# A four-layer metaformer on one core: the expert biases of layer 1 as bfloat16 parts, and one product for the ranks below the diagonal

## The chip, the cores and the metric

The kernel runs on one core of a Trainium2 chip. The metric is the device time of one execution in microseconds; lower is better. A core has five engines with queues of their own: TensorE (PE; its weight loads are listed as PEld), VectorE (DVE), ScalarE (ACT), GpSimd (POOL), and SyncE (SP), which issues most of the transfers. They run side by side and wait for each other by semaphores. Data are worked on in SBUF, 128 partitions wide; TensorE writes its products to PSUM.

## The reference

The program sends 4 x 64 images of 128 x 128 values (256 images) through four layers, each a mixer and a feed-forward part. The change is in layer 1 (the code counts from 0), the second of the four. Its mixer gives every pair (n, m) of rows in an image a weight by the rank of its score among all 128 x 128 scores of the image, and its feed-forward part sends each row to 2 of 8 experts:

```python
ranks = (jnp.argsort(tau, axis=-1) + 1).astype(score.dtype) / n
weights = -jnp.log(ranks).reshape(shp)
...
router_probs = jax.nn.softmax(x @ router_w + router_b, axis=-1)
top_p, top_i = jax.lax.top_k(router_probs, K)
top_p = top_p / jnp.sum(top_p, axis=-1, keepdims=True)
expert_out = jnp.einsum('bnd,edc->bnec', x, expert_w) + expert_b
gathered = jnp.take_along_axis(expert_out, top_i[..., None], axis=2)
return jnp.einsum('bnk,bnkc->bnc', top_p, gathered)
```

So a row's result is the sum over its two experts of gate x (row x expert matrix + expert bias). Everything is float32.

## The kernel before

The layers follow one another through arrays in DRAM. Layer 1 first finds the ranks (distances, then a long sort, lines L1453 to L1833) and leaves them in DRAM as integers, one half of each rank matrix above and one below the diagonal, with a list of tied ranks. Then `l1_blocks` (L1838) does everything else of the layer. It works on 32 blocks of 8 images; most steps are done once for each half block of 4 images, so 64 times.

What a block does, in order of its data:
- `load` and `load_ranks` (L2183, L2187) fetch 8 images and their ranks through SP's queue; `cast` (L2193, GpSimd) turns the ranks into the f32 tiles `above` and `below`.
- `normed` (L1915 to L1981) normalises the images and turns them over by products with the identity.
- `attention`: `tied` (L1991, L1992, VectorE) makes two bfloat16 tiles `ta` and `tb` that place the tied ranks; `ranks` (L1994) adds up the rank matrix of each image in the PSUM tile `pt`: `below` times the identity (L1997), `above` turned over (L1998), and `ta` times `tb` (L1999). All the products of one image follow one another before the next image's. `log` takes the logarithm to `wT`, `values` (L2009) and `product` (L2021) apply the weights, `add` (L2029, L2032) adds to the image.
- `gates`: `route` (L2049) gives the logits; VectorE computes softmax and the choice of two (L2068 to L2091), and `split` (L2094) writes the gates of 8 experts as three bfloat16 parts that add up to the float32 value, `g3` of 3 x 8 values per row.
- `experts`: `turn` (L2114, products L2118) brings the 24 values of each row to 24 partitions, PSUM tile `pl`; ScalarE copies them twice: `keep` to the bfloat16 tile `gb`, `keep_too` (L2126) to the f32 tile `gf`. `spread` (L2137), once for each of the 8 experts, copies an expert's gate to all partitions, as a product of `gb` with the 0/1 matrix `pick`. `times` (L2147) multiplies the images by it: five experts on VectorE, straight from PSUM, three on GpSimd after a copy by ScalarE (L2143). `mixed` (L2159), once per image, adds up in the PSUM tile `pe` the bias, `gf` times `eb3` (L2163: the biases three times over, one for each part of the gate), and the eight products with the expert matrices (L2165). `add` (L2170) adds it to the image, and the block is stored (L2207).

A product of f32 operands stands in the trace as two MATMUL instructions, two passes, each with a weight load; one of bfloat16 operands as one.

The order on TensorE, ScalarE, VectorE and GpSimd isn't that of the code. Each step is given to a planner (`Plan`, L49) with its engine, a cost in microseconds written by hand, the tiles it reads and writes, and those it takes anew. `emit` (L94) goes through them as a list scheduler: always the step that can start first by these costs, given the number of buffers of every tile. The order that results is fixed in the program. By the written costs a block takes 37.6 us of TensorE and 35.0 us of VectorE. Buffers that matter here: `pt` and `pr` two, `pl`, `pv`, `po` and `pe` one each (all PSUM), `xg`, `gb` and `gf` two, and three of most tiles of a block.

Ahead of the blocks lies a setup (L1846 to L1896) that loads the weights through SP's queue, in this order with the blocks' first loads, and makes constants: among them `eb3` (L1875 to L1877), `ones3` and `pick` (L1887 to L1891).

Of the kernel before, what the change touches and what calls it, by code (L numbers as in the profile page):

```python
# [10 lines left out]
F32 = mybir.dt.float32  # L11
I32 = mybir.dt.int32
# [3 lines left out]
BF16 = mybir.dt.bfloat16  # L16
AF = mybir.ActivationFunctionType
ALU = mybir.AluOpType
# [4 lines left out]
P = 128  # L23
B, H, W, C = 4, 64, 128, 128
# [24 lines left out]
class Plan:  # L49
# [16 lines left out]
    def step(self, engine, us, reads, writes, fn, new="", late=0.0):  # L66

        i, deps, holds = len(self.steps), set(), []
        for n in new.split():

            self.last[n] = [set(), None, set()]
            self.users.append((n, self.last[n][0]))
            holds.append(len(self.users) - 1)
            if n in self.turns:
                self.turns[n].append(holds[-1])
        for n in reads.split():
            t = self.last[n]
            t[0].add(i)
            if t[1] is not None:
                deps.add(t[1])  # L80
            t[2].add(i)
        for n in writes.split():
            t = self.last.setdefault(n, [set(), None, set()])
            t[0].add(i)
            deps |= t[2]
            if t[1] is not None:
                deps.add(t[1])
            t[1], t[2] = i, set()
        for n in new.split():
            self.last[n][0].add(i)  # L90
        deps.discard(i)
        self.steps.append((engine, us, deps, holds, fn, late))
# [1745 lines left out]
def l1_blocks(env, x, out, pk, ties, cv, ff):  # L1838

    nc, tc = env.nc, env.tc  # L1840
    NB, E = 8, 8
    with tc.tile_pool(name="ec", bufs=1) as cp, tc.tile_pool(name="es", bufs=3) as sb, tc.tile_pool(
        name="ep", bufs=1, space=PSUM
# [6 lines left out]
        eb = cp.tile([P, 2], F32, name="eb")  # L1850
# [21 lines left out]
        ew = cp.tile([P, E, C], F32, name="ew")  # L1872
        nc.sync.dma_start(ew, ff["expert_w"].rearrange("e d c -> d e c"))

        eb3 = cp.tile([3 * E, C], F32, name="eb3")  # L1875
        for k in range(3):
            nc.sync.dma_start(eb3[E * k : E * k + E, :], ff["expert_b"])  # L1877

        below = cp.tile([P, E, E], F32, name="below")
        nc.vector.memset(below, 0.0)  # L1880
        for i in range(1, E):
# [1 line left out]

        identb = cp.tile([P, P], BF16, name="identb")
        nc.vector.tensor_copy(identb, env.ident)
        ones3 = cp.tile([P, 3, E], F32, name="ones3")
        nc.vector.tensor_copy(ones3, env.ident[:, 0:E].unsqueeze(1).to_broadcast([P, 3, E]))  # L1887
        pp = ps1.tile([3 * E, P], F32, name="pl")
        nc.tensor.matmul(pp, ones3.rearrange("p k e -> p (k e)"), env.ident, start=True, stop=True)
        pick = cp.tile([3 * E, E, P], BF16, name="pick")  # L1890
        nc.vector.tensor_copy(pick, pp[:, 0:E].unsqueeze(2).to_broadcast([3 * E, E, P]))  # L1891
        places = cp.tile([P, P], I32, name="places")
        nc.gpsimd.iota(places, [[1, P]], base=0, channel_multiplier=0)  # L1893
        placeb = cp.tile([P, P], BF16, name="placeb")
# [5 lines left out]
        deep = ["xt", "xT", "xT2", "e", "g", "g3", "mx", "sm", "sn"]  # L1900
        deep += [n + k for n in ("st", "mv", "rs", "nb", "d", "t") for k in "12"]
        plan = Plan(dict(
            gate=DEEP, rt=2, above=2, below=2, xl=2, wT=2, v=2, gt=1, xg=2, gb=2, gf=2, gr=2, ws=2, ta=2, tb=2,
            pt=2, pv=1, po=1, pl=1, pr=2, pe=1, **{n: DEEP for n in deep},
        ), "ta tb wT v gate rt above below xg gb gf gt " + " ".join(deep))
        step = plan.step

        def normed(v, k, tags, eps, name):
# [74 lines left out]
        def attention(v, j0):  # L1983
            w = {}

            def tied():
                w["ta"] = sb.tile([P, 4, P], BF16, name="ta", bufs=2)
                w["tb"] = sb.tile([P, 4, P], BF16, name="tb", bufs=2)
                for j in range(4):
                    col, row, lack = (ties[:, k, v["i"] + j0 + j : v["i"] + j0 + j + 1] for k in range(3))  # L1990
                    V.tensor_scalar(w["ta"][:, j, :], placeb, col, None, ALU.is_equal)  # L1991
                    V.tensor_scalar(w["tb"][:, j, :], placeb, row, lack, ALU.is_equal, ALU.mult)  # L1992

            def ranks():  # L1994
                w["pt"] = ps2.tile([P, 4, P], F32, name="pt")
                for j in range(4):
                    T.matmul(w["pt"][:, j, :], env.ident, v["below"][:, j0 + j, :], start=True, stop=False)  # L1997
                    T.matmul(w["pt"][:, j, :], v["above"][:, j0 + j, :], env.ident, start=False, stop=False)  # L1998
                    T.matmul(w["pt"][:, j, :], w["ta"][:, j, :], w["tb"][:, j, :], start=False, stop=True)  # L1999

            def log():

                w["wT"] = sb.tile([P, 4, P], F32, name="wT", bufs=2)
                S.activation(w["wT"], w["pt"], AF.Ln, scale=1.0 / (W * W))

            def values():
                w["pv"] = ps1.tile([P, 4, C], F32, name="pv")
                for j in range(4):
                    T.matmul(w["pv"][:, j, :], v["xT"][:, j0 + j, :], m, start=True, stop=True)  # L2009

            def keep():

                w["v"] = sb.tile([P, 4, C + 1], F32, name="v", bufs=2)
                G.memset(w["v"][:, :, C : C + 1], 1.0)
                V.tensor_add(w["v"][:, :, 0:C], w["pv"], cst.unsqueeze(1).to_broadcast([P, 4, C]))

            def product(j):
                def f():
                    w["po", j] = ps1.tile([P, 2, 2 * P], F32, name="po")
                    for q in range(2):  # L2020
                        T.matmul(  # L2021
                            w["po", j][:, q, 0 : C + 1], w["wT"][:, j + q, :], w["v"][:, j + q, :], start=True, stop=True
                        )
                return f

            def add(j):
                def f():
                    po, ws = w["po", j], sb.tile([P, 2], F32, name="ws", bufs=2)
                    V.reciprocal(ws, po[:, :, C])  # L2029
                    for q in range(2):  # L2030
                        xj = v["xt"][:, j0 + j + q, :]
                        V.scalar_tensor_tensor(xj, po[:, q, 0:C], ws[:, q : q + 1], xj, ALU.mult, ALU.add)  # L2032
                return f

            step("dve", 1.4, "above", "ta tb", tied, new="ta tb")
            step("pe", 2.4, "above below ta tb", "pt wT", ranks, new="pt wT")
            step("act", 0.6, "pt", "wT", log)
            step("pe", 1.0, "xT_%d" % j0, "pv v", values, new="pv v")
            step("dve", 0.75, "pv", "v", keep)
            for j in range(0, 4, 2):  # L2040
                step("pe", 0.5, "wT v", "po", product(j), new="po")
                step("dve", 0.95, "po xl0 xl4 xm0 xm4", "x1_%d ws" % (j0 + j), add(j), new="ws")

        def gates(v):
# [49 lines left out]
            def split():  # L2094

                g = v["g"]
                v["g3"] = g3 = sb.tile([P, NB, 3, E], BF16, name="g3")
                V.tensor_copy(g3[:, :, 0, :], g)
                V.tensor_sub(g, g, g3[:, :, 0, :])
                V.tensor_copy(g3[:, :, 1, :], g)  # L2100
                V.tensor_sub(g3[:, :, 2, :], g, g3[:, :, 1, :])

            step("dve", 0.5, "", "e mx", shift, new="mx")
            step("act", 0.35, "", "e", lambda: S.activation(v["e"], v["e"], AF.Exp))
# [5 lines left out]
        def experts(v, j0):  # L2110
# [2 lines left out]

            def turn():  # L2114
                w["xg"] = sb.tile([P, E, 4, P], F32, name="xg", bufs=2)
                w["pg"] = ps1.tile([3 * E, 4, P], F32, name="pl")
                for j in range(4):
                    T.matmul(  # L2118
                        w["pg"][:, j, :], v["g3"][:, j0 + j].rearrange("p k e -> p (k e)"), identb, start=True, stop=True
                    )  # L2120

            def keep():
                w["gb"] = sb.tile([3 * E, 4, P], BF16, name="gb", bufs=2)
                S.copy(w["gb"], w["pg"])

            def keep_too():  # L2126
                w["gf"] = sb.tile([3 * E, 4, P], F32, name="gf", bufs=2)
                S.copy(w["gf"], w["pg"])

            step("pe", 0.6, "g3", "pl xg", turn, new="pl xg")  # L2130
            step("act", 0.55, "pl", "gb", keep, new="gb")
            step("act", 0.55, "pl", "gf", keep_too, new="gf")

            def spread(q):
                def f():
# [23 lines left out]
            def mixed(j):  # L2159
                def f():  # L2160
                    if j == 0:
                        w["pe"] = ps1.tile([P, 4, C], F32, name="pe")
                    T.matmul(w["pe"][:, j, :], w["gf"][:, j, :], eb3, start=True, stop=False)  # L2163
                    for q in range(E):
                        T.matmul(w["pe"][:, j, :], w["xg"][:, q, j, :], ew[:, q, :], start=False, stop=(q == E - 1))  # L2165
                return f

            def add():
# [2 lines left out]

            parts = " ".join("xg%d_%d" % (j0, q) for q in range(E))
            for j in range(4):
                step("pe", 2.1, "xg gf " + parts, "pe", mixed(j), new="pe" if j == 0 else "")
            step("dve", 0.7, "pe x1_%d x1_%d xl0 xl4 xm0 xm4" % (j0, j0 + 2), "x2_%d" % j0, add)

        def block(i):
# [1259 lines left out]
```

## Time and profile before

| | |
|---|---|
| median of 3 runs | 12128.36 us (12107.32 to 12131.01) |
| the profiled execution, its own time | 12125.25 us |
| its span, first to last instruction | 12123.1 us |
| mean granted TensorE clock | 0.789 of full |
| busy, whole span | PE 62%, DVE 83%, ACT 62%, POOL 51% |
| stage of the blocks | 5331 to 6715 us |
| largest groups on PE there | L2165 536.0 us busy (x4096), L2137 177.6 (x512), L1997 114.7 (x512), L2163 113.6 (x512) |

The profile is of one execution. Busy time counts an instruction from start to end; the ends of matmuls are modelled and overlap their followers, so where TensorE is tight the distances between starts are the better measure. "out<-in" names the tiles that a group writes and reads; 24*128 after the tiles of a matmul are the rows and columns of the array that it uses. The clock column is the share of full TensorE clock that was granted.

### The profile page before, as it was taken

To read this page: it belongs to the slowest core of one execution; us is meant where nothing else is said; L and a number is where in the kernel's file an instruction comes from. 1 tells how busy PE (TensorE), PEld (TensorE's weight loads), DVE (VectorE), ACT (ScalarE), POOL (GpSimd) and SP (SyncE) were. 2 spreads that over 40 slices of the span, in tenths; PEclk is the share of its full clock that TensorE was granted. 3 is DMA by queue.
4 is the path that set the end of the run, shared out by engine and by line. 5 is a ranking of instruction groups with operands and counts; after the bars stand their busy time and mean duration, and the time that the engine had idled before them with its cause. 6 is when DMAs were issued, how large, how long until landed. Compare 5 with 4: busy or idle time off the path is not lost. (4 is left out here: it accounts for less than half of the span.)

```text
span 12123.1 us, 115274 instructions
## 1 busy us (share of the span) xinstructions
PE 7529.4 (62%) x34606; PEld 4567.5 (38%) x34606; DVE 10007.7 (83%) x16341; ACT 7550.9 (62%) x10927; POOL 6180.6 (51%) x5275
## 2 busy tenths in 40 slices
PE   7887785000000000038999699999899999998765
PEld 5655554000000000027788344444444444446443
DVE  7566638999999999987787699999999999997354
ACT  4355534888867777622333577787777777786332
POOL 1000016999950000002222699999989999995222
PEclk8876798555555555569999899999999999999877
DMA  4223245111111111121111233434333433433434
GB/s 142 83 46 94 72 143 136 56 58 57 58 55 56 56 56 53 40 54 37 38 40 30 103 138 137 142 137 149 133 138 137 141 135 140 144 134 116 177 124 155
DMA packets 632306, 1193.55 MB, mean 98 GB/s; under 512 B 216508, under 2 KB 433902, under 8 KB 552302
## 3 DMA queue, kind: packets, MB, share of 16 engines
q1 hardware_dynamic: 587454, 1042.99, 25.7%
q0 software_dynamic: 34656, 140.92, 3.5%
q8 instruction: 279, 4.57, 0.2%
q10 hardware_dynamic: 9552, 2.08, 0.1%
q14 instruction: 365, 2.99, 0.1%
HBM read 950.86 MB, written 251.71 MB: 99 GB/s over the span
## 5 line engine op out<-in xcount | busy, mean ns | idle before, releaser
L2699 POOL TENSOR_TENSOR gs<-hist,cc 128x512 f32<-128x512 f32 x2048 | 2573.5, 1265 | 382.4 <-DVE hist L2694 237.8
L2694 DVE TENSOR_TENSOR_SCAN hist<-da,state,bs 128x512 f32<-128x512 f32 x1984 | 2524.0, 1272 | 0.0
L2708 PE MATMUL py<-gs,ident 128*128 128x512 f32 x4096 | 2248.1, 631 | 5.8 <-DVE y L2584 5.8
L1633 PE MATMUL pt<-ident,both 128*128 128x128 f32 x6 | 2.7, 445 | 3258.3 <-DVE both L1631 3258.3
L2665 ACT ACTIVATE da<-dt,am 128x512 f32<-128x512 f32 x2048 | 1415.0, 715 | 332.6 <-DVE hist L2694 330.0
L2686 DVE TENSOR_TENSOR bs<-dx,bs 128x512 f32<-128x512 f32 x2048 | 1393.7, 681 | 182.6 <-PE bs L2672 136.1
L1509 POOL TENSOR_TENSOR diff<-key 128x2048 f32<-128x2048 f32 (+11 forms) x364 | 1384.1, 3861 | 87.1 <-DVE key L1514 75.1
L1633 PEld LDWEIGHTS pt<-ident,both 128*128 128x128 f32 x6 | 1.1, 182 | 3259.8 <-issue 3259.8
L2708 PEld LDWEIGHTS py<-gs,ident 128*128 128x128 f32 x4096 | 739.1, 197 | 905.4 <-issue 427.3
L1893 POOL IOTA places<- 128x128 int32 x1 | 0.2, 239 | 1811.4 <-SPq L1833 1811.4
L2672 PE MATMUL bs<-bt,pick 96*128 96x512 bf16 x2048 | 807.2, 394 | 145.1 <-DVE hist L2694 142.1
L1531 ACT COPY keep<-rank 128x1536 int16<-128x1536 int16 (+11 forms) x364 | 612.8, 1686 | 437.5 <-DVE rank L1533 388.8
L1507 ACT COPY low<-key 128x2048 f32<-128x2048 f32 (+11 forms) x364 | 627.7, 1725 | 285.1 <-DVE key L1514 276.0
L1532 DVE COPY_PREDICATED rank<-back,rank 128x1536 int16<-128x1536 uint8 (+11 forms) x364 | 781.6, 2147 | 16.7 <-ACT keep L1531 16.7
L1533 DVE COPY_PREDICATED rank<-back,keep 128x1536 int16<-128x1536 uint8 (+11 forms) x364 | 777.9, 2137 | 12.5
L1513 DVE TENSOR_TENSOR key<-low,key 128x2048 f32<-128x2048 f32 (+11 forms) x364 | 749.3, 2059 | 6.9 <-DMA key<-dist 4.4
L1514 DVE TENSOR_TENSOR key<-low,key 128x2048 f32<-128x2048 f32 (+11 forms) x364 | 744.5, 2045 | 12.4
L1510 ACT ACTIVATE turned<-diff 128x2048 int8<-128x2048 f32 (+11 forms) x364 | 600.5, 1699 | 36.5 <-DMA key<-dist 27.4
L1522 ACT ACTIVATE back<-turned 128x3072 uint8<-128x3072 int8 (+12 forms) x182 | 582.5, 3200 | 0.0
L2165 PE MATMUL pe<-ew,xg 128*128 128x128 f32 x4096 | 536.0, 285 | 1.7 <-DVE xg L2147 1.7
L2165 PEld LDWEIGHTS pe<-ew,xg 128*128 128x128 f32 x4096 | 486.0, 195 | 34.0 <-DVE xg L2147 2.5
L2147 POOL TENSOR_TENSOR xg<-xT,gr 128x512 f32<-128x512 f32 x192 | 245.3, 1278 | 473.1 <-ACT gr L2143 472.9
(815 smaller groups left out, 18624.6 us busy)
## 6 DMA issues: line engine op xcount, KB each, us to landing
cc<-cd SPq DMA_DIRECT2D x512, 1024.0 KB
xt<-state SPq DMA_DIRECT2D x64, 1024.0 KB
xo<-state SPq DMA_DIRECT2D x128, 256.0 KB
state<-xo POOLq DMA_DIRECT2D x128, 256.0 KB, 2.8
xl<-in_L_ffn_weight SPq DMA_DIRECT2D x32, 1024.0 KB
tk<-in_x SPq DMA_DIRECT2D x32, 512.0 KB
tokens<-tt POOLq DMA_DIRECT2D x32, 512.0 KB, 4.8
tk<-tokens SPq DMA_DIRECT2D x8, 2048.0 KB
```

The source lines that it names most:

```text
L1509: nc.gpsimd.tensor_sub(d, lo[part], hi[part])
L1513: nc.vector.tensor_tensor(lo[part], c, hi[part], ALU.min)
L1514: nc.vector.tensor_tensor(hi[part], c, hi[part], ALU.max)
L1532: nc.vector.copy_predicated(l, t, h)
L1533: nc.vector.copy_predicated(h, t, kv)
L2165: T.matmul(w["pe"][:, j, :], w["xg"][:, q, j, :], ew[:, q, :], start=False, stop=(q == E - 1))
L2665: nc.scalar.activation(da, x_["dt%d" % b], AF.Exp, scale=am[:, s : s + 1])
L2672: nc.tensor.matmul(bs, pick[:, s, :], x_["bt%d" % b], start=True, stop=True)
L2686: nc.vector.tensor_mul(db, x_["dx%d" % b], db)
L2694: nc.vector.tensor_tensor_scan(h, live.pop(("da", t)), live.pop(("db", t)), 0.0 if first else state[b][:, s : s + 1], ALU.mult, ALU.add,)
L2699: nc.gpsimd.tensor_tensor(gs, h, live.pop(("cc", t)), ALU.mult)
L2708: nc.tensor.matmul(x_["py%d" % b], env.ident, live.pop(("gs", t)), start=(s == 0), stop=(s == S - 1))
```

## The change

Three things are edited, all in `l1_blocks`.

Biases. `eb3` (f32, 24 rows) becomes `eb9` (bfloat16, 72 rows): each bias is split into three bfloat16 parts that add up to it, and part l stands in rows 24 l to 24 l + 23, three times over. It is made in the setup, from nine loads of `expert_b` in place of three and some 15 small instructions. `split` writes the three parts of the gates three times, so that every part of a gate meets every part of a bias; `turn`, `gb` and `pick` get 72 rows in place of 24 (the rows of `pick` from 24 on are zero, so `spread` computes what it did). The f32 copy `gf` and its step are gone. `mixed` adds the bias of all four images as four bfloat16 products ahead of the first image's expert products, and the accumulation in `pe` is begun once and ended once for the four.

Ranks. `below` times the identity is one product of 512 columns for the four images in place of four of 128; then come the four of `above`, then the four of `ta` and `tb`.

Planner. The cost of `ranks` is 2.2 in place of 2.4, `keep_too` is gone, and `mixed` waits for `gb` in place of `gf`.

```diff
-        eb3 = cp.tile([3 * E, C], F32, name="eb3")
-        for k in range(3):
-            nc.sync.dma_start(eb3[E * k : E * k + E, :], ff["expert_b"])
+        R = 9 * E
+        eb9 = cp.tile([R, C], BF16, name="eb9")
+        with tc.tile_pool(name="eb", bufs=1) as bp:
...
+            for k in range(9):
+                nc.sync.dma_start(left[E * k : E * k + E, :], ff["expert_b"])
+            row = bp.tile([R, 1], I32, name="row")
+            nc.gpsimd.iota(row, [[1, 1]], base=0, channel_multiplier=1)
...
+            for l in range(3):
+                nc.vector.tensor_copy(part, left)
+                nc.vector.tensor_sub(left, left, part)
+                nc.vector.scalar_tensor_tensor(ebs, part, sel[:, l : l + 1], ebs, ALU.mult, ALU.add)
+            nc.vector.tensor_copy(eb9, ebs)
...
-        pick = cp.tile([3 * E, E, P], BF16, name="pick")
-        nc.vector.tensor_copy(pick, pp[:, 0:E].unsqueeze(2).to_broadcast([3 * E, E, P]))
+        pick = cp.tile([R, E, P], BF16, name="pick")
+        nc.vector.tensor_copy(pick, pp[:, 0:E].unsqueeze(2).to_broadcast([R, E, P]))
...
             def ranks():
                 w["pt"] = ps2.tile([P, 4, P], F32, name="pt")
+                T.matmul(w["pt"], env.ident, v["below"][:, j0 : j0 + 4, :], start=True, stop=False)
                 for j in range(4):
-                    T.matmul(w["pt"][:, j, :], env.ident, v["below"][:, j0 + j, :], start=True, stop=False)
                     T.matmul(w["pt"][:, j, :], v["above"][:, j0 + j, :], env.ident, start=False, stop=False)
-                    T.matmul(w["pt"][:, j, :], w["ta"][:, j, :], w["tb"][:, j, :], start=False, stop=True)
+                for j in range(4):
+                    T.matmul(w["pt"][:, j, :], w["ta"][:, j, :], w["tb"][:, j, :], start=False, stop=(j == 3))
...
-            step("pe", 2.4, "above below ta tb", "pt wT", ranks, new="pt wT")
+            step("pe", 2.2, "above below ta tb", "pt wT", ranks, new="pt wT")
...
-                v["g3"] = g3 = sb.tile([P, NB, 3, E], BF16, name="g3")
-                V.tensor_copy(g3[:, :, 0, :], g)
-                V.tensor_sub(g, g, g3[:, :, 0, :])
-                V.tensor_copy(g3[:, :, 1, :], g)
-                V.tensor_sub(g3[:, :, 2, :], g, g3[:, :, 1, :])
+                gs = g.unsqueeze(2).to_broadcast([P, NB, 3, E])
+                v["g3"] = g3 = sb.tile([P, NB, 3, 3, E], BF16, name="g3")
+                V.tensor_copy(g3[:, :, :, 0, :], gs)
+                V.tensor_sub(g, g, g3[:, :, 0, 0, :])
+                V.tensor_copy(g3[:, :, :, 1, :], gs)
+                V.tensor_sub(g3[:, :, :, 2, :], gs, g3[:, :, :, 1, :])
...
-                w["gb"] = sb.tile([3 * E, 4, P], BF16, name="gb", bufs=2)
+                w["gb"] = sb.tile([R, 4, P], BF16, name="gb", bufs=2)
                 S.copy(w["gb"], w["pg"])
...
-            step("act", 0.55, "pl", "gf", keep_too, new="gf")
...
                     if j == 0:
                         w["pe"] = ps1.tile([P, 4, C], F32, name="pe")
-                    T.matmul(w["pe"][:, j, :], w["gf"][:, j, :], eb3, start=True, stop=False)
+                        for q in range(4):
+                            T.matmul(w["pe"][:, q, :], w["gb"][:, q, :], eb9, start=(q == 0), stop=False)
                     for q in range(E):
-                        T.matmul(w["pe"][:, j, :], w["xg"][:, q, j, :], ew[:, q, :], start=False, stop=(q == E - 1))
+                        T.matmul(w["pe"][:, j, :], w["xg"][:, q, j, :], ew[:, q, :], start=False, stop=(j == 3 and q == E - 1))
...
-                step("pe", 2.1, "xg gf " + parts, "pe", mixed(j), new="pe" if j == 0 else "")
+                step("pe", 2.1, "xg gb " + parts, "pe", mixed(j), new="pe" if j == 0 else "")
```

More of the change, by code (lines that the diff above doesn't have):

```diff
@@ L1873, in l1_blocks @@
         nc.sync.dma_start(ew, ff["expert_w"].rearrange("e d c -> d e c"))
-        eb3 = cp.tile([3 * E, C], F32, name="eb3")
-        for k in range(3):
-            nc.sync.dma_start(eb3[E * k : E * k + E, :], ff["expert_b"])
+        R = 9 * E
+        eb9 = cp.tile([R, C], BF16, name="eb9")
+        with tc.tile_pool(name="eb", bufs=1) as bp:
+            left, part, sel = bp.tile([R, C], F32, name="left"), bp.tile([R, C], BF16, name="part"), bp.tile([R, 3], F32, name="sel")
+            ebs = bp.tile([R, C], F32, name="ebs")
+            for k in range(9):
+                nc.sync.dma_start(left[E * k : E * k + E, :], ff["expert_b"])
+            row = bp.tile([R, 1], I32, name="row")
+            nc.gpsimd.iota(row, [[1, 1]], base=0, channel_multiplier=1)
+            rowf = bp.tile([R, 1], F32, name="rowf")
+            nc.vector.tensor_copy(rowf, row)
+            nc.vector.tensor_scalar(sel[:, 0:1], rowf, float(3 * E), None, ALU.is_lt)
+            nc.vector.tensor_scalar(sel[:, 2:3], rowf, float(6 * E), None, ALU.is_ge)
+            nc.vector.tensor_tensor(sel[:, 1:2], sel[:, 0:1], sel[:, 2:3], ALU.add)
+            nc.vector.tensor_scalar(sel[:, 1:2], sel[:, 1:2], -1.0, 1.0, ALU.mult, ALU.add)
+            nc.vector.memset(ebs, 0.0)
+            for l in range(3):
[3 more added lines that the diff above has]
+            nc.vector.tensor_copy(eb9, ebs)
         below = cp.tile([P, E, E], F32, name="below")
@@ L1885, in l1_blocks @@
         nc.vector.tensor_copy(identb, env.ident)
[L1886 to L1889, printed above, removed]
-        pick = cp.tile([3 * E, E, P], BF16, name="pick")
-        nc.vector.tensor_copy(pick, pp[:, 0:E].unsqueeze(2).to_broadcast([3 * E, E, P]))
+        ones9 = cp.tile([P, 9, E], F32, name="ones9")
+        nc.vector.memset(ones9, 0.0)
+        nc.vector.tensor_copy(ones9[:, 0:3, :], env.ident[:, 0:E].unsqueeze(1).to_broadcast([P, 3, E]))
+        pp = ps1.tile([R, P], F32, name="pl")
+        nc.tensor.matmul(pp, ones9.rearrange("p k e -> p (k e)"), env.ident, start=True, stop=True)
+        pick = cp.tile([R, E, P], BF16, name="pick")
+        nc.vector.tensor_copy(pick, pp[:, 0:E].unsqueeze(2).to_broadcast([R, E, P]))
         places = cp.tile([P, P], I32, name="places")
@@ L1902, in l1_blocks @@
         plan = Plan(dict(
-            gate=DEEP, rt=2, above=2, below=2, xl=2, wT=2, v=2, gt=1, xg=2, gb=2, gf=2, gr=2, ws=2, ta=2, tb=2,
+            gate=DEEP, rt=2, above=2, below=2, xl=2, wT=2, v=2, gt=1, xg=2, gb=2, gr=2, ws=2, ta=2, tb=2,
             pt=2, pv=1, po=1, pl=1, pr=2, pe=1, **{n: DEEP for n in deep},
-        ), "ta tb wT v gate rt above below xg gb gf gt " + " ".join(deep))
+        ), "ta tb wT v gate rt above below xg gb gt " + " ".join(deep))
         step = plan.step
@@ L2115, in turn @@
                 w["xg"] = sb.tile([P, E, 4, P], F32, name="xg", bufs=2)
-                w["pg"] = ps1.tile([3 * E, 4, P], F32, name="pl")
+                w["pg"] = ps1.tile([R, 4, P], F32, name="pl")
                 for j in range(4):
                     T.matmul(
-                        w["pg"][:, j, :], v["g3"][:, j0 + j].rearrange("p k e -> p (k e)"), identb, start=True, stop=True
+                        w["pg"][:, j, :], v["g3"][:, j0 + j].rearrange("p l k e -> p (l k e)"), identb, start=True, stop=True
                     )
             def keep():
-                w["gb"] = sb.tile([3 * E, 4, P], BF16, name="gb", bufs=2)
+                w["gb"] = sb.tile([R, 4, P], BF16, name="gb", bufs=2)
                 S.copy(w["gb"], w["pg"])
-            def keep_too():
-                w["gf"] = sb.tile([3 * E, 4, P], F32, name="gf", bufs=2)
-                S.copy(w["gf"], w["pg"])
             step("pe", 0.6, "g3", "pl xg", turn, new="pl xg")
             step("act", 0.55, "pl", "gb", keep, new="gb")
-            step("act", 0.55, "pl", "gf", keep_too, new="gf")
             def spread(q):
```

## The prediction

> **What bounds the kernel now.** The page comes first. Its chain of waits names no line with more than a rounded 0% and is no help for a stage in the middle, so I cut the stage out by lines: everything the diff touches runs from 5331 us (first product for `pt`) to 6715 us (last store), 32 blocks of 8 images. The busy time of each engine in stretches of that stage:
> ```profile
> core 0: us, PE busy (x) PEld busy (x) DVE busy (x) ACT busy (x) POOL busy (x), PEclk, DMA share, GB/s
> 5655.50:5747.60 92.10, 81.16 (x576) 67.74 (x576) 66.01 (x215) 26.35 (x58) 21.82 (x22) 0.91 0.13 36
> 5880.00:6600.00 720.00, 703.40 (x5233) 589.49 (x5232) 574.22 (x1916) 235.06 (x527) 194.81 (x198) 1.00 0.14 39
> ```
> From 5880 us on TensorE is busy 98% at full clock, and the stores of the blocks are 39.6 us apart: TensorE is the bound there. VectorE is busy 80%, 31.6 us of each 39.6; ScalarE and GpSimd a third or less. Before 5880 us two blocks take about 92 us, 46 each: once in a pair TensorE runs dry behind VectorE, and the clock is granted at half for some 17 us after it. The waits say who stands behind whom (columns: total us, times, longest), first of 5400 to 6000, then of 6000 to 6600 us:
> ```profile
> PE pl L2118 <- DVE g L2101: 26.0, 4, 8.6
> ...
> DVE xg L2147 <- PE pr L2137: 45.7, 45, 2.4
> DVE xt L2170 <- PE pe L2165: 35.2, 31, 1.7
> DVE v L2015 <- PE pv L2009: 12.7, 16, 0.8
> ```
> In the later 600 us (15.2 blocks) VectorE's idle time is its wait for TensorE: with `ws` (7.1) and `sm` (4.8) 105.5 us, 7 us a block. So time taken off TensorE comes off the block until VectorE is full.
>
> Third, TensorE's own timeline (columns: start, busy, line, tile, count); starts matter, not the modelled ends:
> ```profile
> 6012.64 0.39 PE L1998 MATMUL pt<-ident,above 128*128 128x128 f32 x2
> 6012.86 0.22 PE L1999 MATMUL pt<-tb,ta 128*128 128x128 bf16 x1
> 6013.01 0.48 PE L2163 MATMUL pe<-eb,gf 24*128 24x128 f32 x2
> 6013.42 2.05 PE L2165 MATMUL pe<-ew,xg 128*128 128x128 f32 x16
> 6015.41 0.38 PE L2137 MATMUL pr<-gb,pick 24*128 24x512 bf16 x1
> 6015.63 0.38 PE L2163 MATMUL pe<-eb,gf 24*128 24x128 f32 x2
> 6015.94 2.05 PE L2165 MATMUL pe<-ew,xg 128*128 128x128 f32 x16
> ```
> An f32 product is two passes; 128 columns start 0.112 us apart (14 of the 15 steps inside L2165). The two passes of the bias, L2163, take 0.41 us at 6013.01 where 0.22 is their own: their 24 rows differ from the neighbours' 128, and 0.20 pass between the last bias pass and L2165, and 0.21 between L2165's first two. What a row count does is seen in the next layer:
> ```profile
> 6854.10 1.12 PE L2708 MATMUL py<-gs,ident 128*128 128x512 f32 x2
> 6855.06 0.38 PE L2672 MATMUL bs<-bt,pick 96*128 96x512 bf16 x1
> 6855.37 1.13 PE L2456 MATMUL pa<-xn,wconv 64*128 64x512 f32 x4
> 6856.43 1.12 PE L2708 MATMUL py<-gs,ident 128*128 128x512 f32 x2
> ```
> 96 rows to 64 costs 0.31 us after a 512-column bfloat16 product; 96 rows straight to 128 (L2672 to L2708) 0.215 to 0.220, the same as no change; [...]. So a change between the 64-row and full shapes costs 0.09 us, and 96 rows count as full. I take 72 rows, over 64 too, as full.
>
> [...] in this trace an f32 pass of 512 columns takes 0.428 us and one of 256 takes 0.215, [...]
>
> **The change, part by part** (per half block of 4 images, at full clock, 64 of them).
>
> Ranks, L1997 to L1999. Before: 0.556 us per image (starts 6005.62, 6006.22, 6006.78, 6007.33 less one change), 2.22 in all. After: one product of 512 columns is 2 x 0.43, not a quarter of four, since f32 passes are paid by the column; then 8 x 0.112 for `above`, and four bfloat16 passes, which cost 0.11 now because an f32 load follows each, at 3 x 0.056 + 0.11. Sum 2.04: 0.19 saved, nearly all by the regrouping of bfloat16.
>
> Bias, L2163. Before, per image: 0.174 between its passes on average, 0.200 to L2165, 0.10 more than usual inside L2165's first pair, and the entry at 0.093 or, behind L2137, 0.010, mean 0.06. Together 0.54, 2.15 for four. After: four bfloat16 passes of 0.056 at full shape and one f32 load behind them, 0.28. Saved: 1.87.
>
> Spread, L2137, from 24 rows to 72, still 512 columns, 0.216 each. Of its 8 in a half block 5.1 enter from a full shape, 0.094 each: 0.48. Exits to L2118, L2009 and L1997 are 1.56 at 0.09: 0.14; those to L1969 and L2021 end in waits, so I count none of their 0.18. [...] makes the first f32 pair behind it 0.1 longer: 0.30 in the half block. Sum 0.92, with 0.6 and 1.1 as ends.
>
> Turn, L2118: 24 output columns become 72. Its own changes (0.093 at entry and exit, about half the time each) vanish, 0.10; [...] Net 0.06.
>
> TensorE sum: 0.19 + 1.87 + 0.92 + 0.06 = 3.04 a half block, 6.1 a block; 39.6 - 6.1 = 33.5 us are left.
>
> ScalarE: the copy to `gf`, 64 x 573 ns = 36.7 us, goes; ScalarE is a third busy, so I count nothing. The PSUM tile `pl` comes free 0.57 us sooner.
>
> VectorE, `split`: four instructions of 64 elements (193, 225, 195, 225 ns) become two casts and one subtraction of 192 elements and one of 64. Rows of 64 and 512 elements (225 and 689 ns) give about 1.04 ns an element: 3 x 128 x 1.04 = 0.40 us a block, 13 us over 32. It hides in the 7 us of VectorE's waits; without that cover, as in the early pairs, TensorE stands behind `g3` and it costs its 0.40.
>
> Setup: six more loads of `expert_b` on SP's queue, ahead of the first `xt` and `rt`. The three of before start 0.50 us apart (5328.84, next load 5330.33), so the first blocks' loads come 3.0 us later, and the first product waits for `rt`: +3. About 17 small VectorE instructions of 0.1 to 0.3 us end at about 5338, when `xt` lands anyway. GpSimd's small iota is off the path. If the chain came last instead: up to +5.
>
> **What the block becomes.** TensorE 33.5; VectorE 31.6 + 0.4, with 1 us of gaps that no wait explains, 33. Two engines this equal, with single buffers of `pl`, `pe`, `pv` and `po` between them and an order fixed in advance by the planner's own costs (ranks 2.4 to 2.2 and `keep_too` gone, so it will be another order), don't reach the larger sum. I take 35.5 us, 4.1 saved, between 37.5 and 33.8. In the early pairs 92 us become 84.3: the dry stretch, which VectorE sets, and the half clock stay, and of the 12.2 saved on TensorE in a pair I take 7.7 off: 3.85 a block.
>
> Sum on the profiled execution (12125.25 us; span 12123.1): 19 x 4.1 + 13 x 3.85 - 3 = 125, to 12000. The median of the runs is 3 us higher than that execution: 12003.
>
> **Rivals.**
> - The stage stays as now, in pairs and then level, with the gain half lost to VectorE (0.64, the forecast; its own range 11955 to 12050).
> - VectorE becomes the bound at once: its queue is in order, and each late `g3` or `x2` stops TensorE. For it speaks that it is 80% full now; against, that its waits are for TensorE. A block of 38 us, 1.6 saved: 32 x 1.6 - 3 = 48, 12080 (0.15). I put 4 of these 15 chances within 0.2% (24 us).
> - The new order has no pairs: all 32 blocks at 34.5. The stage, 1375 us with some 35 of ends, becomes 1139: -236 and +3, 11895 (0.11). For it: half of the blocks now waste 6 us in dry stretches that are a matter of order alone.
> - Slower: TensorE, with 6 us less to do, runs dry behind `g` [...] in every block, not every second, and each costs 17 us at half clock, 8.5 lost. 33.5 + 8.5 + 5 dry = 47 a block against 42.2 on average now: +153 us, 12280. It decides from 8.7 us lost a block on. For it: the pairs show the mechanism. Against: during the half clock VectorE catches up, and at full clock 19 blocks in a row show none (0.10).
> - That it doesn't do what it says: [...] Then 0.92 and part of the bias stay, 4 a block is the saving of TensorE, perhaps 3 of the block: 12035, inside the forecast's range. The 96 rows speak against it; its chance is in the first.
>
> **Numbers.** Chances: faster by over 0.2% (24 us, about what a measurement here tells from none) 0.64 + 0.11 + 0.11 = 0.86; within 0.04; slower 0.10. The likeliest case gives 12003. The range from 11900 to 12085 takes in the second rival and most of the third, and leaves out the slow one.
>
> **What would show it.** L2163's successor at 256 bfloat16 instructions, 0.056 apart, and no 0.2 us step between it and L2165; L2137 to an f32 product at 0.22, not 0.30; L1997 at 128 instructions 0.43 apart. Stores 35 to 36 us apart in the level part, VectorE's wait for `pr` and `pe` halved. Wrong, if the stores stay over 38 us apart with TensorE idle behind VectorE, or if the half clock spreads.

## The result and the profile after

The changed kernel takes 11940.57 us (median of 4 runs, 11934.11 to 11953.21) against 12129.69 us before: a ratio of 0.9845, interval 0.9834 to 0.9857. That is 189 us less; 125 were forecast, and the range held it. The profiled execution took 11937.16 us, its span 11935.4.

The whole difference lies in the stage of the blocks. Its last store moved from 6709.9 to 6517.4 us, by 192.5; what follows it lasts 5413.2 and 5418.0 us. The times of the blocks' stores show two gains (an interval is the time from one block's store to the next):

| stretch of the stage | before | after | difference | forecast |
|---|---|---|---|---|
| to the first store | 5436.0 | 5431.8 | -4.2 | about -1 (setup +3, first block -3.85) |
| 11 intervals that follow | 486.0 | 383.6 | -102.4 | about -42 |
| 18 level intervals | 713.4 | 637.9 | -75.5 | -74 |
| last 2 | 74.5 | 64.1 | -10.4 | -8 |

The level intervals went from 39.6 to 35.4 us; 35.5 was the forecast. But the early pairs, which were to shrink, are gone: the interval is 35.4 from the second on. The engines' busy time in stretches of the kernel after, with the columns of before:

```profile
core 0: us, PE busy (x) PEld busy (x) DVE busy (x) ACT busy (x) POOL busy (x), PEclk, DMA share, GB/s
5431.80:5815.40 383.60, 357.55 (x2906) 319.93 (x2906) 349.30 (x1143) 131.04 (x294) 116.64 (x119) 1.00 0.16 46
5815.40:6453.30 637.90, 594.72 (x4826) 530.90 (x4825) 576.99 (x1892) 216.94 (x487) 189.08 (x194) 1.00 0.15 42
```

Both stretches run at full clock and at the same shares: TensorE 93%, VectorE 91%, where it was 98% and 80% in the level part before. TensorE's timeline of the kernel after (start, busy, engine, line, tiles, count):

```profile
5861.31 0.39 PE L2181 MATMUL pe<-eb,gb 72*128 72x128 bf16 x4
5861.53 2.00 PE L2183 MATMUL pe<-ew,xg 128*128 128x128 f32 x16
5863.37 0.38 PE L2154 MATMUL pr<-gb,pick 72*128 72x512 bf16 x1
5863.59 1.95 PE L2183 MATMUL pe<-ew,xg 128*128 128x128 f32 x16
5865.38 0.38 PE L2154 MATMUL pr<-gb,pick 72*128 72x512 bf16 x1
```

Four images' bias takes 0.22 us, from 5861.31 to L2183 at 5861.53, where one image's took 0.41. The spread is followed by L2183 after 0.22: 72 rows are a full shape. Who makes TensorE wait, 5460 to 6460 us (total us, times, longest):

```profile
PE pt L1989 <- DVE xl L1977: 35.4, 56, 0.7
PE pl L2140 <- DVE g L2123: 12.4, 28, 0.5
PE pr L2154 <- ACT gr L2160: 8.8, 30, 0.7
PE po L2042 <- DVE v L2036: 7.4, 26, 0.3
```

Twice in each of the 28 blocks of this stretch TensorE now waits for `xl`, once for the gates `g`. Before, in the level part, it hardly waited at all: VectorE waited for it. VectorE's waits for `pr` and `pe`, 45.7 and 35.2 us in 600 us before, are 2.9 us and none in these 1000.

Below, an interval is that of the stores in the level part of one profiled execution. It repeats to 0.1 us (35.4 here and where only the biases' loads were moved), while what lies around the stage shifts from run to run: the time behind the last store was anything from 5394.3 to 5436.1 us in the profiled runs. The times of whole kernels carry that too, those of single runs above all.

### The profile page after: what moved, and what is told of

It reads as the page before. It is cut to its first block, busy times and chain, and to the rows that moved or that the text cites. A ratio compares the mean times of both kernels' runs of the same rounds, so it can differ in the third digit from the quotient of the medians.

```text
span 11935.4 us, 113939 instructions
## 1 busy us (share of the span) xinstructions
PE 7337.1 (61%) x33966; PEld 4454.9 (37%) x33966; DVE 10014.6 (84%) x16358; ACT 7522.4 (63%) x10863; POOL 6182.3 (52%) x5276
## 5 line engine op out<-in xcount | busy, mean ns | idle before, releaser
L2183 PE MATMUL pe<-ew,xg 128*128 128x128 f32 x4096 | 504.4, 277 | 0.0
L2183 PEld LDWEIGHTS pe<-ew,xg 128*128 128x128 f32 x4096 | 488.2, 193 | 3.9
```

## The experiments

**Where did the pairs go? Order and instructions apart.** Two kernels cross the two. One has the changed instructions, planned as before:

```diff
...
-            step("pe", 2.2, "above below ta tb", "pt wT", ranks, new="pt wT")
+            step("pe", 2.4, "above below ta tb", "pt wT", ranks, new="pt wT")
...
+            step("act", 0.55, "pl", "gf", lambda: None, new="gf")
...
-                step("pe", 2.1, "xg gb " + parts, "pe", mixed(j), new="pe" if j == 0 else "")
+                step("pe", 2.1, "xg gf " + parts, "pe", mixed(j), new="pe" if j == 0 else "")
```

> The changed instructions in the order of the kernel before: the planner is given ranks at 2.4 and a ScalarE step of 0.55 that issues nothing, so that it plans as before. Theory A (the pairs of before are a matter of the planned order): the first 11 to 13 blocks come in pairs again, about 84 us a pair, the rest 35.4 us apart; 12000 to 12020. Rival B (the pairs went because TensorE has less to do): level at 35.4 from the start, about 11940.

The pairs came back: intervals of 47.6 and 31.6, then 48.9 and 31.6, then 35.4 from the twelfth on. The first 11 intervals sum to 428.2 us. Ratio to before 0.9875 (0.9851 to 0.9899), median 11964.45, below the 12000 to 12020 expected: a pair took 80 us and not 84, and the kernel before ran 17 us faster beside it (12112.67) than in the first comparison. The largest of TensorE's waits in this kernel, 5431 to 5828 us:

```profile
PE pl L2140 <- DVE g L2123: 29.8, 9, 8.7
```

and the busy times of that stretch:

```profile
5431.00:5828.00 397.00, 344.58 (x2666) 306.05 (x2666) 322.05 (x1046) 121.53 (x270) 108.68 (x110) 0.92 0.14 41
```

The dry stretch behind `g`, up to 8.7 us, and the half clock (0.92 in the mean) are those of before.

The other has the instructions of before in the new order:

```diff
...
-            step("pe", 2.4, "above below ta tb", "pt wT", ranks, new="pt wT")
+            step("pe", 2.2, "above below ta tb", "pt wT", ranks, new="pt wT")
...
                 S.copy(w["gb"], w["pg"])
-
-            def keep_too():
                 w["gf"] = sb.tile([3 * E, 4, P], F32, name="gf", bufs=2)
                 S.copy(w["gf"], w["pg"])
...
-            step("act", 0.55, "pl", "gf", keep_too, new="gf")
...
-                step("pe", 2.1, "xg gf " + parts, "pe", mixed(j), new="pe" if j == 0 else "")
+                step("pe", 2.1, "xg gb " + parts, "pe", mixed(j), new="pe" if j == 0 else "")
```

> The instructions of before in the order of the changed kernel: ranks planned at 2.2, both copies of ScalarE in one step, all products as before. Theory A (order): no pairs, all blocks about 39.6 us apart, some 56 us off: 12060 to 12085. Rival B (less work for TensorE): pairs as before, 12130.

No pairs: 39.6 from the second interval on. Ratio 0.9946 (0.9925 to 0.9967), median 12049.0, 64 us below the kernel before beside it where some 56 were expected. So the pairs are a matter of the order alone, whatever the instructions.

**Which edit made the order.** The kernel before, with the first pair of lines of that diff and nothing else:

> The kernel before with one number changed: the planner's cost of ranks, 2.4 to 2.2. Every instruction is that of before. If this number alone makes the order: level at 39.6 us from the second block, no half clock after 5420 us, 12045 to 12070, the same as with both of ScalarE's copies in one step. Rival (the missing ScalarE step is needed too): pairs stay, 12120.

Ratio 0.9954 (0.9938 to 0.9971), median 12062.06; intervals of 39.6 from the second on. In the same stretch as above:

```profile
5431.00:5828.00 397.00, 387.57 (x2871) 324.83 (x2870) 315.46 (x1053) 128.89 (x291) 108.12 (x110) 1.00 0.14 41
```

Full clock, TensorE 98% busy. A hand-written cost that no instruction sees, moved by 0.2 us, took 55 us off the 11 early intervals (486.0 to 431.1) and 51 off the kernel's median.

What the order does can be read from the traces. From the last logits of a block (L2049) to the first product that turns its gates (L2118), in the kernel before:

```profile
5645.60 1.06 PE L2049 MATMUL pl<-rw,xT 128*128 128x128 f32 x8
...
5660.80 0.60 PE L2118 MATMUL pl<-identb,g 128*24 128x128 bf16 x4 [8.56 <-DVE g L2101]
```

and in the kernel with the one cost changed:

```profile
5598.84 1.06 PE L2049 MATMUL pl<-rw,xT 128*128 128x128 f32 x8
...
5608.79 0.39 PE L2118 MATMUL pl<-identb,g 128*24 128x128 bf16 x4
```

In this early block of the old order VectorE takes 13.5 us over the gates (L2056 at 5647.26 to the end of L2101 at 5660.75): steps of `tied`, `add` and `normed` stand between theirs, and two of the comparisons take 1.3 and 1.5 us in place of 0.7. Between logits and turn TensorE has 5.5 us of other work. In the new order VectorE does the gates in one go, in 7.2 us (5599.93 to 5607.16), and TensorE has 8.9 us of work behind which they hide; so it is in the level part of the kernel before. Apart from the copy to `gf`, the traces show TensorE, ScalarE, VectorE and GpSimd going through the blocks in the order of the kernel before in the first of these three kernels, and in that of the changed kernel in the other two.

**The price of the shapes.** The changed kernel, with `spread` on the 24 rows that hold something:

```diff
-                    T.matmul(w["pr", q], pick[:, q, :], w["gb"], start=True, stop=True)
+                    T.matmul(w["pr", q], pick[0 : 3 * E, q, :], w["gb"][0 : 3 * E], start=True, stop=True)
```

> The changed kernel, but spread uses rows 0 to 23 of pick and gb alone (the others are zero in pick): the same order, the same 512 columns, only the row count of L2137's successor is 24 again. If a change of array shape costs 0.09 us each way: TensorE +1.84 us a block, stores 36.4 to 37.3 us apart, 32 to 60 us slower than the changed kernel. Rival (the row count is free and the bias alone saved): 35.4 as it is.

Interval 36.7, 1.3 us more, within the range expected. The one run took 11952.41 us, only 12 more than the changed kernel's median where 32 to 60 were expected; from the first store to the last it is 43.6 us longer (1129.2 against 1085.6), and what follows the stage happened to be 23.7 shorter. The profile of this kernel:

```profile
5874.82 0.38 PE L2154 MATMUL pr<-gb,pick 24*128 24x512 bf16 x1
5875.14 2.05 PE L2183 MATMUL pe<-ew,xg 128*128 128x128 f32 x16
5877.12 0.39 PE L2154 MATMUL pr<-gb,pick 24*128 24x512 bf16 x1
5877.44 2.05 PE L2183 MATMUL pe<-ew,xg 128*128 128x128 f32 x16
```

0.32 from the spread to L2183 in place of 0.22, and 1.98 from there back to the spread in place of 1.79: of the 0.19, 0.09 is the change back and 0.10 the first f32 pair, whose weights aren't loaded ahead: their load starts with the product (5875.14), where in the changed kernel it starts with the spread (5863.37), 0.22 before the product. Behind the 24 rows of the bias in the kernel before, load and product start together too (L2165, both at 6015.94). All three terms of the forecast are there. The interval grew by less than their 1.84 because TensorE's waits around `xl` shrank: by its starts, the products that turn the images over (L1989), and the steps from the spread into them, take 4.39 us a block here and 5.32 in the changed kernel; everything else takes 2.2 more.

**The price of the bias.** The changed kernel with the f32 bias back:

```diff
+        eb3 = cp.tile([3 * E, C], F32, name="eb3")
+        for k in range(3):
+            nc.sync.dma_start(eb3[E * k : E * k + E, :], ff["expert_b"])
...
                 S.copy(w["gb"], w["pg"])
+                w["gf"] = sb.tile([3 * E, 4, P], F32, name="gf", bufs=2)
+                S.copy(w["gf"], w["pg"][0 : 3 * E])
...
-                        for q in range(4):
-                            T.matmul(w["pe"][:, q, :], w["gb"][:, q, :], eb9, start=(q == 0), stop=False)
+                    T.matmul(w["pe"][:, j, :], w["gf"][:, j, :], eb3, start=True, stop=False)
...
```

> The changed kernel with its bias undone: a second ScalarE copy to an f32 tile of 24 rows in the same step, and per image the f32 product with the three copies of the biases. Same order. Theory (the bias was 1.87 us of TensorE a half block): stores 38 to 39 us apart, 85 to 115 us slower than the changed kernel. Rival (VectorE bounds the changed kernel, so that most of the bias's time was given away): under 36.5 us, under 35 us slower.

Interval 39.2, 3.8 us more, just above the 38 to 39 expected: the bias was not given away to VectorE. One run, 12034.6 us, 94 more than the changed kernel's median.

**The price of the ranks.** The kernel before with the new `ranks`, planned at 2.4 as before:

> The kernel before with the new order of products in ranks alone, planned as before. By f32 passes that are paid by the column: level stores 39.6 - 0.38 = 39.2 us apart, about 12 us faster. Rival (one product of four images costs a quarter of four products): 0.67 us less a half block, 38.3 us apart, about 43 us faster.

39.2 in place of 39.6, the pairs as they were; one run, 12114.3 us against a median of 12125.53 for the kernel before beside it, whose runs spread over 31 us. One product of 512 f32 columns saves what was worked out from passes paid by the column, and no more: its two passes start 0.43 us apart in the changed kernel (L2016), where those of 128 columns start 0.11 apart.

**What bounds the kernel after.** First, four of VectorE's eight scalings to ScalarE, with the planner told:

```diff
-                affine((0, 2), V)()
+                affine((0,), V)()
...
-                    step("dve", 0.7, tags(4) + scales + "xl", "xl4", affine((4, 6), V))
-                step("act", 1.0, tags(j0) + scales + "xl", "xm%d" % j0, affine((j0 + 1, j0 + 3), S))
+                    step("dve", 0.35, tags(4) + scales + "xl", "xl4", affine((4,), V))
+                step("act", 1.5, tags(j0) + scales + "xl", "xm%d" % j0, affine((j0 + 1, j0 + 2, j0 + 3), S))
```

> The changed kernel with four of VectorE's eight scalings a block (0.49 us each) given to ScalarE: VectorE -2.0 us a block, ScalarE +2.0, TensorE the same; the planner is told (0.35 and 1.5 for 0.7 and 1.0). Theory C (VectorE and TensorE bound the changed kernel together): stores 34.0 to 34.6 us apart, 25 to 45 us faster than the changed kernel, about 11905. Rival D (TensorE and the fixed order alone): 35.4 +- 0.2, no gain.

Theory C missed: 35.4 in the level part, long intervals again among the first four (38.5, 49.8, 39.7), ratio 0.9858 (0.9842 to 0.9875). The wait had moved. In the kernel of this run, 5700 to 6200 us, `xl` is no longer waited for, but the routers' `pl`, of which there is one buffer, is:

```profile
PE pl L2070 <- DVE e L2077: 11.0, 14, 0.8
PE pl L2140 <- DVE g L2123: 6.2, 14, 0.4
PE pl L2070 <- ACT xT L2001: 5.7, 14, 0.4
```

The told costs had made another order, so this run mixes two things. The next keeps the planner's old 0.7 and 1.0 and moves the same work:

> As the scaling moved to ScalarE before, but the planner is told nothing, so that the order is that of the changed kernel. VectorE up to 2.0 us a block less, in front of the gates and not in their chain. Theory E: no pairs at the start, stores 35.1 to 35.4 us apart, within 10 us of the changed kernel. Rival C (VectorE's total counts, and the last try lost it to its new order): 34.0 to 34.6, 25 to 45 us faster.

34.6, no pairs, one run of 11894.69 us, 46 less than the changed kernel's median. That is the upper end of theory C's range for the interval, and theory E as I had put it, the gates' chain alone, falls. But 0.8 us a block came off where VectorE lost more than twice that, so C's total isn't the whole account either. The third kernel shortens that chain, again in the changed kernel's order:

```diff
-        below = cp.tile([P, E, E], F32, name="below")
+        below = cp.tile([P, E, E], BF16, name="below")
...
-                v["gt"] = gt = sb.tile([P, 2, NB, E, E], F32, name="gt", bufs=1)
+                v["gt"] = gt = sb.tile([P, 2, NB, E, E], BF16, name="gt", bufs=1)
```

> The changed kernel with the comparisons of the gates (gt, 0 or 1, and the constant below) in bfloat16, in the same order. It shortens the chain from the last logits to g3, [...]. Theory E (the level spacing of the changed kernel is a loop: TensorE's work plus its wait for this chain): stores 34.7 to 35.0 us apart, 12 to 22 us faster than the changed kernel, about 11920. Rival (TensorE alone): 35.4, no gain.

34.9, ratio 0.983 (0.9814 to 0.9846), median 11909.57. Of the chain's five instructions of 0.69 us, two (L2105, L2110) take 0.425 us each in this kernel, 0.53 less together. TensorE's waits in this kernel, 5460 to 6460 us, with no line for `g`:

```profile
PE pt L1989 <- DVE xl L1977: 35.3, 56, 0.7
PE po L2042 <- POOL v L2035: 9.0, 27, 1.2
```

and in the one with the scalings moved:

```profile
PE pl L2140 <- DVE g L2123: 19.9, 29, 7.6
PE pt L1989 <- DVE xl L1977: 19.8, 28, 0.7
```

The first took the wait for `g` away, the second one of the two waits for `xl` in each block (the 19.9 holds a single wait of 7.6; the rest is as before). So the level interval of the changed kernel is TensorE's work plus separate waits for VectorE, for `xl` and for `g`.

**The setup.** The nine loads of the biases on another queue:

```diff
-                nc.sync.dma_start(left[E * k : E * k + E, :], ff["expert_b"])
+                nc.scalar.dma_start(left[E * k : E * k + E, :], ff["expert_b"])
```

> The changed kernel with the nine loads of the biases issued from ScalarE's queue in place of SP's, nothing else. If the six loads more on SP delay the first blocks: first product for pt at about 5339 us in place of 5342.6, the whole 3 to 4 us earlier; else unchanged.

By the distance from the setup's last product to the first of `pt`, in the changed kernel

```profile
5331.51 0.70 PE L1909 MATMUL pl<-ident,ones 128*72 128x128 f32 x2 [0.38 <-DVE cst L1864]
5342.61 2.08 PE L2016 MATMUL pt<-below,ident 128*128 128x512 f32 x2 [10.40 <-POOL below L2211]
```

it is 11.1 us, and 8.2 in this kernel (5325.51 to 5333.71): 2.9 us earlier. The absolute times differ by more because the layers ahead ended sooner in that run. The whole time of one run, 11933.6 us, can't show 3 us.

**Together.** The last three in one kernel, of which the edits are those shown:

> The three that helped the changed kernel, together: comparisons of the gates in bfloat16, four scalings a block on ScalarE in the same order, the biases' loads on ScalarE's queue. If TensorE's two waits in a block (for the gates' chain and for xl) are separate, their shares add: 35.4 - 0.5 - 0.8 = 34.1 us between stores, 31 x 1.3 + 3 = 43 us faster than the changed kernel, about 11895. If one wait only takes the place of the other: 34.6, some 25 us faster.

34.1: the shares add. Ratio to before 0.9804 (0.979 to 0.9817), median 11901.53 of 5 runs. Its interval lies below that of the changed kernel's ratio, so this is faster than the changed kernel as well as the kernel before.

## Why the prediction was right, and where it was not

*The bound.* Right: before, TensorE alone set the level part, and its time came off the block until VectorE was nearly full: 4.2 us a block where 4.1 was the forecast.

*Ranks, -0.38 us a block.* The run gave -0.4.

*Bias, -3.74.* The interval gave 3.8 with the bias undone. It is not a pure price: there 24 rows stand among full shapes everywhere, also behind the spread (0.31 us from it to the bias), and TensorE's wait for `g` is gone.

*Spread, -1.84 and turn, -0.12.* The single steps are as worked out: 0.22 from the spread to L2183 where 24 rows take 0.32, 0.11 into the spread where they take 0.21, and 0.11 inside the first f32 pair where it is 0.21. The interval grew by 1.3 with 24 rows back. The forecast's net of 0.06 a half block for `turn` is the 0.10 of its shape changes less 0.04 for longer loads, an estimate of mine that no trace showed. It wasn't needed: the products of `turn` start 0.056 us apart as before, and so do the four of the bias, each with a load of 128 columns.

*VectorE, +0.40.* The four instructions of `split` take 1.13 us (259, 226, 260, 389 ns), 0.30 more than the 0.84 of before.

*The setup, +3.* The first product of `pt` came at 5342.6, not 5339.4 (the 5331 of the prediction is where TensorE begins to wait for it), and moving the loads gave 2.9 back. The first store is 4.2 us earlier all the same, since the first block is shorter too.

*The level block, 35.5.* 35.4: TensorE is busy for 33.0 of it (594.72 of 637.9 us) and idle for 2.4. What I gave as the reason, two nearly equal engines with single buffers, was too coarse: named waits make it up, and taking away the one for `g`, or one of the two for `xl`, shortened the block.

*The pairs, 92 to 84.3 us: this step failed.* With the old order the changed instructions take 80 us a pair, so its price of the shorter instructions was near. But I wrote that it would be another order, and then carried the pairs over from the old one. The two early stretches are 11 intervals long; of their 102 us, 58 are the shorter instructions within the pairs (486.0 to 428.2 in the old order) and 45 the order (428.2 to 383.6); taken the other way round, 55 are the order (486.0 to 431.1) and 48 the instructions. So the forecast fell short by 64 us, most of it this term. The third rival, no pairs at 34.5 us a block, had its mechanism right and its block one us too short; 0.11 was too little for it. The profile of before doesn't say whether the new order has pairs, and a chance nearer a half for either would have been fair. But the order is made by code of the kernel from written costs alone, so it could have been listed for the new costs and laid beside the old one, to see what work stands between logits and gates.

*The slow rival* did not come about, but its mechanism did, where the scalings were moved and the planner told: costs that follow the moved work (0.35 and 1.5) gave an order with dry stretches in its first blocks, and a granted clock of 0.86 in the mean of the longest one (5491 to 5541 us). It had also been priced too high. Of the 17 us at half clock in a pair, from about 5655.5 to 5672.5, five lie within the dry stretch, which ends at 5660.8; the other 12 lose some 6 us of TensorE's work, not 8.5 (the products of `turn` start 0.107 us apart there, and 0.056 at full clock). How long TensorE has to stand idle before the clock falls was not shown; in this pair the half clock begins some 3.2 us after the end of its last product (5652.24).

## What to carry to other kernels

Read the price of a small matmul from the starts around it: a bias of 24 rows took 0.22 us of its own passes, and 0.3 more on average in changes of shape and late weights. Here 72 rows, 48 of them zeros, were cheaper for the spread than 24 among full products (0.22 us to the next product in place of 0.32). Where a planner's costs make the order, an edit to a cost is a change of its own with a time of its own: run it alone, and hold the order fixed when anything else is to be measured. Then look at how much other work the order leaves an engine while it waits for a chain on another.

## What the runs showed of the hardware that was not expected

VectorE's scalings of 128 f32 elements from SBUF to SBUF have two durations. In the stage of the changed kernel 199 of them ran beside no GpSimd product and took 0.341 us in the median (0.330 to 0.347); 56 ran beside such products of 512 f32 elements for nine tenths of their length or more and took 1.08 us (28 of them) or 1.41 (28). Both kinds in its timeline:

```profile
5868.40 1.11 DVE L1977 TENSOR_SCALAR xl<-xt,rs,nb 128x128 f32<-128x128 f32 x4
...
5870.52 2.60 POOL L2164 TENSOR_TENSOR xg<-xT,gr 128x512 f32<-128x512 f32 x2 [4.74 <-ACT gr L2160]
5870.79 2.92 DVE L1977 TENSOR_SCALAR xl<-xt,rs,nb 128x128 f32<-128x128 f32 x4
5872.02 0.68 PE L1989 MATMUL pt<-ident,xl 128*128 128x128 f32 x4 [0.71 <-DVE xl L1977]
```

Four scalings take 1.11 us alone and 2.92 beside the two products, and TensorE's wait for `xl` stands right behind. Each of the 56 ends 0.080 to 0.086 us after a GpSimd product does, as if it had waited for that end. Why a scaling takes longer there was not shown, and no run of its own put the scalings apart from the products. The long scalings would explain why the move of four of them helped although VectorE's total was not the bound: with the order kept, the 28 of 1.41 us are gone there and 28 of 1.08 are left.

VectorE's product of two bfloat16 tiles (L2105, 512 elements) took 0.425 us in the kernel with the gates' comparisons in bfloat16, where f32 took 0.692; the comparison of f32 inputs to a bfloat16 output (L2103) stayed at 0.691.
